# A ViT tower on one core: other tokenizer groups, masked remainder rows, and a hand-ordered start of the linear attention

## The chip, the cores and the metric

The kernel is written for one NeuronCore of a Trainium2 chip and runs on that core alone. The metric is the device time of one execution in microseconds (us). An execution has several engines that each take their instructions in order: TensorE (PE, with its weight loads listed as PEld), VectorE (DVE), ScalarE (ACT), GpSimd (POOL) and SyncE (SP), which issues most of the transfers; they wait for each other through semaphores.

## The reference, cut to what matters

Four images give 784 tokens of 256 numbers each, all in fp32. The tokens pass a tokenizer and two pre-norm layers, each of attention and a mixture of experts; each part is added to its input `h`.

```
# tokenizer
t = layernorm(layernorm(patches) @ W1 + b1)
h = silu(layernorm([t, t, t] @ Wp1 + bp1)) @ Wp2 + bp2
# layer 0: softmax attention, then top-2 of 6 experts
h = h + attention0(layernorm(h));  h = h + experts0(layernorm(h))
# layer 1: linear attention
q, k, v = split(layernorm(h) @ W_qkv + b_qkv), q and k centred
q2 = q*q / (sum(q*q) + 1e-7), then divided by its norm over the channels
k2 = k*k / (sum(k*k) + 1e-7), then divided by its norm over the TOKENS of the image
kv = k2^T @ v;  h = h + (v + q2 @ kv / sqrt(N)) @ W_out + b_out
# layer 1: shared MLP and top-2 of 4 experts
h = h + mlp1(layernorm(h))
```

The images in the output are written three times over (REP = 3). The norm of k2 over the tokens and `kv` are sums over all 784 tokens of one image: these are the sums that the change touches.

## The kernel before

**Rows.** An image is 784 = 6 * 128 + 16 rows. Its six full tiles of 128 rows are tiles 0 to 23 for the four images together; the four remainders of 16 rows share one more tile, LT = 24, the "left" tile, image b at partitions 32*b to 32*b + 15. The rows between hold values that belong to no token.

**Order.** The code records operations; a scheduler then places them on the engines. Inside `manual_schedule(engines=...)` the named engines keep the order of the code, and only there; operations recorded later, outside such a block, may still be put between those of the block. PSUM is a pool of 7 banks, and `copy_out` (L82) and `bias_relu` (L90) give their work in turn to ACT and DVE, by one counter that both share.

**Tokenizer (36 to 111 us).** It goes through the tiles in groups (L305): the first has tiles 0, 1, 2 and LT, seven more have three tiles each. For a group, `first_steps` (L537) multiplies the patches by Wall (`pw`, L547), copies half of the result to y on ACT (L550), takes statistics on DVE (L551), a square root on ACT (L556), y times r plus bp1 on DVE (L562), statistics, a second square root on ACT (L569) and the normalised rows xn on DVE (L573). `turned_rows` (L579) transposes xn on PE (`pt`, L274) and applies silu on ACT (L585). `last_rows` (L602) multiplies by Wp2 (`pwp`, L294) and adds the bias into h. `tokenize` (L594) takes these as a pipeline: group g's first steps, g - 1's turn, g - 2's last rows. The last group and the one before it are put in a fixed order on DVE, PE and ACT (from L634), and the layer norm of the next layer for the first group (`second_norm`, L615) is recorded ahead of the last groups. Silu and square root use different tables of ACT, so that the trace has a row ACT_TABLE_LOAD at each switch.

**Layer 1, linear attention (476 to 612 us).** The rows are units: units 0 to 7 have three tiles each, two units an image, and unit LU = 8 is the left tile. The outputs of layer 0's experts lie in DRAM (`yrows`). `fetch` (L1522) gathers them: for each tile two gathers, issued by POOL, into a buffer `ys` of which there are three. `stats_one` (L1539) waits for the two gathers, multiplies them by the routing weights, adds them to h (two DVE operations, L1545) and takes statistics (L1554, L1555). `normalise` (L1557) writes the normalised rows xa (L1568). `x_t` transposes xa (lxT, copied out by L86 and L88). `q_k` (L1734) multiplies by W_qkv (`pqk`, L1750), adds the bias on DVE (L1754) and squares on ACT. `scales` (L1765) computes the scale of each row and applies it to k on ACT (uk) and to q on DVE (L1781). `fold` (L1788) sums the squares of uk. `q_t` transposes the scaled q (lqT). `k_x` (L1809), once an image, sums over the image's tokens on PE: `pn` (L1816, L1817) for the norm, and `pukx`, uk transposed times xa, as two groups of six matmuls over the full tiles (L1829) and one over the image's 16 rows of the left tile (L1833). Their scaled result g (L1837) is transposed (`g_t`), multiplied by Wv·Wout (`kv_out`, L1853), and `rows_out` (L1867) adds the unit's result to h (`pout`, L1874, L1879). `layer1_weights` (L712) makes the products of the weights that this needs, and a bias `bout` that `residual` (L1575) adds to h.

The gathers for units 0, 1, LU and 2 are recorded inside the expert loop before, those for 3 and later in the loop from L1902, which takes the units in a software pipeline. That loop is left to the scheduler.

**Layer 1, mixture of experts (612 us to the end).** Four groups of four tiles and three of three; the matmuls `ps1`, `pe1`, `pe2`, `ps3` with relus by `bias_relu`, and the output transfers of each tile.

Of the kernel before, what the change touches and what calls it, by code (L numbers as in the profile page):

```python
# [27 lines left out]
P = 128  # L28
TT = 128
# [36 lines left out]
def tile_vit_tower(ctx: ExitStack, tc: tile.TileContext, a: dict, out: bass.AP):  # L66
# [59 lines left out]
    nc.gpsimd.memset(live, 0.0)  # L126
    for b in range(NI):
        nc.gpsimd.memset(live[b * SEG : b * SEG + LEFT], 1.0)

# [176 lines left out]
    groups[0].append(LT)  # L306

# [229 lines left out]
    def first_steps(g):  # L537

        tiles = groups[g]
        n = len(tiles)  # L540
        y = tokp.tile([TT, GT, D], F32, tag="y", name="y", bufs=2)
        st = small.tile([TT, GT, 6], F32, tag="st", name="st")
        mv = small.tile([TT, GT, 2], F32, tag="mv", name="mv")
        for j in range(n):
            pm = ps_tile("pw1")[:TT]
            for c in range(2):
                nc.tensor.matmul(  # L547
                    pm, pixels(c, tiles[j]), Wall[:, c, :], start=(c == 0), stop=(c == 1)
                )
            nc.scalar.copy(y[:, j, :], pm[:, D:])  # L550
            nc.vector.bn_stats(st[:, j, :], pm[:, :D])  # L551
            nc.vector.bn_aggr(mv[:, j, :], st[:, j, :])
        r = small.tile([TT, GT], F32, tag="rstd", name="rstd")[:, :n]
        nc.vector.tensor_tensor(r, mv[:, :n, 0], mv[:, :n, 0], ALU.mult)
        nc.vector.tensor_tensor(r, r, mv[:, :n, 1], ALU.add)
        nc.scalar.activation(r, r, AF.Sqrt, bias=zero[:TT])  # L556
        nc.vector.reciprocal(r, r)
        yield
        st = small.tile([TT, GT, 6], F32, tag="st", name="st")
        mv = small.tile([TT, GT, 2], F32, tag="mv", name="mv")  # L560
        for j in range(n):
            nc.vector.scalar_tensor_tensor(  # L562
                y[:, j, :], y[:, j, :], r[:, j : j + 1], bp1, ALU.mult, ALU.add
            )
            nc.vector.bn_stats(st[:, j, :], y[:, j, :])
            nc.vector.bn_aggr(mv[:, j, :], st[:, j, :])
        yield
        r = small.tile([TT, GT], F32, tag="rstd", name="rstd")[:, :n]
        nc.scalar.activation(r, mv[:, :n, 1], AF.Sqrt, bias=eps[:TT])  # L569
        nc.vector.reciprocal(r, r)  # L570
        xn = tokw.tile([TT, GT, D], F32, tag="xn", name="xn", bufs=3)
        for j in range(n):
            nc.vector.tensor_scalar(  # L573
                xn[:, j, :], y[:, j, :], mv[:, j, 0:1], r[:, j : j + 1],
                ALU.subtract, ALU.mult,
            )
        normed[g] = xn

    def turned_rows(g):  # L579
        xn = normed.pop(g)  # L580
        n = len(groups[g])
        xT = tokw.tile([P, 2, GN], F32, tag="xTt", name="xTt")

        def put(c, pt):
            nc.scalar.activation(  # L585
                xT[:, c, : n * TT], pt, AF.Silu, scale=col("lnp_g", c), bias=col("lnp_b", c)
            )

        transposed(xn, n, put)
        return xT  # L590
# [3 lines left out]
    def tokenize(g):  # L594
        if g < len(groups):
            first_rows(g)
        if 1 <= g <= len(groups):
            third[g - 1] = turned_rows(g - 1)
        if g >= 2:
            last_rows(g - 2)  # L600

    def last_rows(g):  # L602
        sT = third.pop(g)
        tiles = groups[g]
# [23 lines left out]
    n = len(groups)  # L628
# [83 lines left out]
    def layer1_weights():  # L712
        WvT = w1p.tile([P, 2, D], F32, tag="WvT", name="WvT")
        pt = ps_tile("pwv").rearrange("p (k i) -> p k i", k=2)
        for k in range(2):
            for c in range(2):
# [3 lines left out]
                )  # L720
        nc.vector.tensor_copy(WvT, pt)
        Wvo = w1p.tile([P, 2, D], F32, tag="Wvo", name="Wvo")
# [8 lines left out]
        bvs = w1p.tile([P, 2, P], F32, tag="bvs", name="bvs")  # L731
        for k in range(2):
            nc.vector.tensor_copy(bvs[:, k, :], col("bv", k).to_broadcast([P, P]))
# [7 lines left out]
        return Wvo, bvo, bres  # L741
# [775 lines left out]

    for xa in (*xas, xaL):
        nc.gpsimd.memset(xa[:, :, D : D + 2], 1.0)
# [37 lines left out]
    def normalise(u):  # L1557
        if u >= len(units):
            return
        b, j0, n = units[u]  # L1560
        t0 = b * TPI + j0
        st, mv = stats.pop(u)
        r = small.tile([TT, GT], F32, tag="rstd", name="rstd")
        nc.scalar.activation(r[:, :n], mv[:, :n, 1], AF.Sqrt, bias=eps[:TT])
# [7 lines left out]
        if lw:  # L1572
            residual(u)

# [6 lines left out]
    def x_t(u):  # L1581
# [7 lines left out]
        transposed(xa_of(u), n, lambda c, pt: copy_out(xT[:, c, : n * TT], pt))  # L1589
# [144 lines left out]
    def q_k(u, j0, j1):  # L1734

        n = units[u][2]
        xT = xTs[u]
        if j0 == 0:
# [4 lines left out]
            )  # L1743
        qk = qks[u]
        ss, s4 = sumsof[u]
        junk = lin.tile([TT, D], F32, tag="junk", name="junk", bufs=1)
        for j in range(j0, min(j1, n)):
            pqk = ps_tile("pqk")[:TT]
            for c in range(2):
                nc.tensor.matmul(  # L1750
                    pqk, xT[:, c, cut(j, 1)], Wqkv[:, c, : 2 * D],
                    start=(c == 0), stop=(c == 1),
                )
            nc.vector.tensor_tensor(qk[:, j, :], pqk, bqkv[:, : 2 * D], ALU.add)  # L1754

            for i in range(2):
                half = qk[:, j, i * D : (i + 1) * D]
                nc.scalar.activation(half, half, AF.Square, accum_out=ss[:, j, i : i + 1])  # L1758
            nc.scalar.activation(junk, qk[:, j, :D], AF.Square, accum_out=s4[:, j : j + 1])
            if 0 < u < LU - 1:  # L1760
                stats_one(u + 1, j)
        if j1 >= n and 0 < u < LU - 1:
            normalise(u + 1)

    def scales(u):  # L1765

        b, j0, n = units[u]
        qk = qks[u]
        ss, s4 = sumsof.pop(u)

        nc.vector.tensor_scalar(ss[:, :n], ss[:, :n], 1e-7, None, ALU.add)
        nc.scalar.activation(s4[:, :n], s4[:, :n], AF.Sqrt, bias=zero[:TT])
# [3 lines left out]
        nc.vector.reciprocal(ss[:, :n], ss[:, :n])  # L1776
        uk = uks[u] = own_of(lin, u, [TT, UT, D], "uk", 3)
        sq = own_of(lin, u, [TT, UT, D], "sq", 1)
        for j in range(n):
            nc.scalar.activation(uk[:, j, :], qk[:, j, D:], AF.Copy, scale=ss[:, j, 1:2])  # L1780
            nc.vector.tensor_scalar(  # L1781
                qk[:, j, :D], qk[:, j, :D], ss[:, j, 0:1], None, ALU.mult
            )
        for j in range(n):
            nc.scalar.activation(sq[:, j, :], uk[:, j, :], AF.Square)
        return sq

# [11 lines left out]
    def q_t(u):  # L1799
# [7 lines left out]
        transposed(qks.pop(u), n, lambda c, pt: copy_out(qT[:, c, : n * TT], pt))  # L1807

    def k_x(b):  # L1809

        acc = sums.pop(b)
        own = slice(b * SEG, b * SEG + LEFT)
        pn = psum_s.tile([P, 512], F32, tag="pss", name="pn")
        for c in range(2):
            of_c = slice(c * P, (c + 1) * P)
            nc.tensor.matmul(pn[:, c : c + 1], acc[:, of_c], ones[:TT], start=True, stop=False)  # L1816
            nc.tensor.matmul(  # L1817
                pn[:, c : c + 1], squares[LU][own, 0, of_c], ones[own], start=False, stop=True
            )
        kn = small.tile([P, 2], F32, tag="kn", name="kn")  # L1820
        nc.scalar.activation(kn, pn[:, :2], AF.Sqrt, scale=float(REP), bias=zero)
        nc.vector.tensor_scalar(kn, kn, 1e-12, None, ALU.max)
        nc.vector.reciprocal(kn, kn)
        g = gs[b] = lin.tile([P, 2, D + 2], F32, tag="g", name="g")
        for c in range(2):
            pg = ps_tile("pukx")[:, : D + 2]
            for j in range(TPI):
# [4 lines left out]
                )  # L1832
            nc.tensor.matmul(  # L1833
                pg, uks[LU][own, 0, c * P : (c + 1) * P], xaL[own, 0, : D + 2],
                start=False, stop=True,
            )
            nc.vector.tensor_scalar(  # L1837
                g[:, c, :], pg, kn[:, c : c + 1], REP / math.sqrt(REP * SEQ),
                ALU.mult, ALU.mult,
            )  # L1840

# [61 lines left out]
    for u in range(LU + 2):  # L1903
        b, odd = divmod(u - 2, 2)
        one_image = u >= 2 and not odd
        if u == 0:
            fetch(3)
            x_t(1)
            q_k(0, 0, UT)
            squares[0] = scales(0)  # L1910
            fold(0, squares.pop(0))
            continue
# [7 lines left out]
        if u == 2:  # L1920
            gT = g_t(0)
            kv_out(0, gT)
            rows_out(0)
            x_t(2)
        if u == 1:
            stats_one(LU, 0)
            normalise(LU)
        if u < LU:
            q_k(u, 0, 2)
        if u == 1:  # L1930
            x_t(LU)
        if one_image and b:
            gT = g_t(b)
        if u < LU:
            q_k(u, 2, UT)
            if u == 1:
                q_k(LU, 0, 1)
                lw.extend(layer1_weights())
                Wvo, bvo = lw[:2]
            squares[u] = scales(u)  # L1940
            if u == 1:
                squares[LU] = scales(LU)
                q_t(LU)
        if one_image and b:
# [5 lines left out]
        if 2 <= u < LU - 1:  # L1950
            x_t(u + 1)
        if u == 3:
            for k in (0, 1, 2, LU):
                residual(k)
        if u >= 2 and (b or odd):
            rows_out(u - 2)
# [109 lines left out]
```

## Time and profile before

| what | value |
|---|---|
| runs of the kernel | 783.15, 783.83, 780.32 us; median 783.15 |
| the profiled execution's own time | 784.6 us |
| its span in the trace | 782.9 us |
| mean granted clock of TensorE | 0.965 |

The profile is of one execution. A page of it has the busy time of each engine, the span in 40 slices, the chain of work that ended last, and the costliest groups of instructions. From the trace come further views: the waits of a stretch (who waited for whom, in all, how often, and the longest), the timeline of an engine (start, duration, engine, line, operation, output <- inputs, count, and in brackets the idle time before it with what ended it), and a table of windows (each engine's busy time and instructions in a stretch, then the granted clock, the share of DMA engines busy, and GB/s). Instructions of one engine overlap a little in the trace: a row of 0.48 us may start 0.40 us after the one before, so that sums of rows are made with the distance between starts where it is known.

### The profile page before, as it was taken

How to read it: one execution, taken by the hardware profiler on the slowest of the kernel's cores; microseconds unless marked ns; L12 is line 12 of the kernel's file. 1: busy time of each engine (PE TensorE's matmuls, PEld its weight loads, DVE VectorE, ACT ScalarE, POOL GpSimd, SP SyncE). 2: the span in 40 equal slices, each digit the busy share in tenths (PEclk: the TensorE clock that was granted, in tenths of full speed). 3: DMA queues.
4: the chain of work that ended last, by engine and by line, in shares of the span. 5: the costliest groups of instructions: out<-in, count | busy, mean ns of one | idle time of the engine just before them, and what ended most of it. 6: DMA issues, size and time to landing. Idle time of an engine off the chain costs nothing.

```text
span 782.9 us, 10611 instructions
## 1 busy us (share of the span) xinstructions
PE 722.2 (92%) x3408; PEld 496.6 (63%) x3408; DVE 483.2 (62%) x1519; ACT 338.3 (43%) x787; POOL 127.7 (16%) x217
## 2 busy tenths in 40 slices
PE   7888889999888779999999998699999999999996
PEld 4745455666555458888888884566676775554653
DVE  4676776778779763456446666789855545444441
ACT  0547875554663654342223325416445612222221
POOL 5300000000073407600033004770000000000000
PEclk9899999999999689999999999799999999999999
DMA  8399999000020663433244324330000013223333
GB/s 205 88 418 417 418 418 412 5 0 1 0 75 33 239 232 121 162 108 90 87 137 131 99 79 129 102 95 20 1 0 2 1 23 96 82 64 100 104 108 108
DMA packets 57749, 98.07 MB, mean 125 GB/s; under 512 B 6407, under 2 KB 47598, under 8 KB 57694
## 3 DMA queue, kind: packets, MB, share of 16 engines
q1 hardware_dynamic: 51184, 80.96, 29.2%
q0 software_dynamic: 5632, 14.58, 6.1%
q10 hardware_dynamic: 878, 1.86, 1.0%
q8 instruction: 27, 0.44, 0.2%
q14 instruction: 28, 0.23, 0.1%
HBM read 31.50 MB, written 65.88 MB: 124 GB/s over the span
## 4 chain that ended last, share of the span: by engine, by line
PE 72%; DVE 16%; ACT 8%; issue 2%; DMA 1%; POOL 0%; DVEq 0%; ACTq 0%; POOLq 0%
PE pb L1321 13%; PE pyb L1338 6%; PE pe L283 6%; PE ps L283 4%; PE pqk L1750 4%; PE pkv L283 4%; PE pt L274 4%; PE pukx L1829 3%; PE ps L2016 3%; PE pout L1874 3%; PE pout L1879 3%; DVE oT L842 3%; PE pwp L294 2%; PE pwo L294 2%; PE ptp L344 2%
## 5 line engine op out<-in xcount | busy, mean ns | idle before, releaser
L1031 POOL DMA_INDIRECT xrows<-xn,pos x50 | 56.4, 1128 | 245.9 <-ACT kq L782 191.0
L1531 POOL DMA_INDIRECT ys<-yrows,pos x52 | 52.8, 1015 | 145.6 <-DMA yrows<-yb 130.6
L1321 PE MATMUL pb<-xTb,own 128*128 128x256 f32 x240 | 59.0, 390 | 3.4 <-DVE r L891 1.8
L1327 ACT ACTIVATE hb<-pb,own 128x256 f32<-128x256 f32 x74 | 35.1, 475 | 55.3 <-PE pb L1321 48.6
L1321 PE MATMUL pb<-hb,own 128*128 128x256 f32 x240 | 57.0, 380 | 0.3 <-DVE hb L1329 0.3
L1338 PE MATMUL pyb<-own,hb 128*128 128x256 f32 x240 | 57.1, 380 | 0.0
L1321 PEld LDWEIGHTS pb<-xTb,own 128*128 128x128 f32 x240 | 44.7, 194 | 11.8 <-issue 1.9
L274 PE MATMUL pt<-ident,xn 128*128 128x128 f32 x200 | 33.9, 296 | 17.6 <-DVE xn L573 11.1
L1338 PEld LDWEIGHTS pyb<-own,hb 128*128 128x128 f32 x240 | 45.4, 190 | 6.5 <-ACT hb L1327 0.4
L1750 PE MATMUL pqk<-Wqkv,lxT 128*128 128x512 f32 x100 | 46.5, 611 | 0.9 <-ACT lxT L86 0.9
L1321 PEld LDWEIGHTS pb<-hb,own 128*128 128x128 f32 x240 | 43.4, 190 | 5.9 <-DVE hb L1329 0.7
L274 PEld LDWEIGHTS pt<-ident,xn 128*128 128x128 f32 x200 | 25.1, 149 | 34.0 <-ACT y L550 10.4
L1344 DVE TENSOR_TENSOR yb<-pyb,eb 128x512 f32<-128x512 f32 x30 | 20.7, 691 | 41.2 <-PE pyb L1338 41.2
L283 PE MATMUL pe<-xT,eW 128*128 128x512 f32 (+1 forms) x112 | 46.0, 553 | 0.0
L1311 ACT COPY xTb<-ptb 128x512 f32<-128x512 f32 x30 | 17.5, 584 | 63.4 <-PE ptb L1307 63.4
L547 PE MATMUL pw<-Wall,pT 128*128 128x512 f32 x96 | 42.8, 593 | 0.0
L1329 DVE TENSOR_SCALAR hb<-pb,own 128x256 f32<-128x256 f32 x46 | 22.1, 482 | 28.7 <-PE pb L1321 28.6
L807 DVE SCALAR_TENSOR_TENSOR prod<-kq 128x784 f32<-128x784 f32 x32 | 30.4, 972 | 6.0 <-ACT kq L1165 3.4
L283 PEld LDWEIGHTS pe<-xT,eW 128*128 128x128 f32 x112 | 20.2, 190 | 21.6 <-issue 16.5
L1750 PEld LDWEIGHTS pqk<-Wqkv,lxT 128*128 128x128 f32 x100 | 18.7, 194 | 22.0 <-issue 17.3
L1298 DVE COPY own<-ew 128x1540 f32 x30 | 29.0, 965 | 4.9 <-issue 1.6
L1758 ACT ACTIVATE qk<-qk 128x256 f32<-128x256 f32 x50 | 20.3, 407 | 23.7 <-DVE qk L1754 21.4
(394 smaller groups left out, 1481.2 us busy)
## 6 DMA issues: line engine op xcount, KB each, us to landing
xrows<-nothing SPq DMA_DIRECT2D x22, 896.0 KB
yrows<-nothing SPq DMA_DIRECT2D x22, 896.0 KB
out_dram<-h SPq DMA_DIRECT2D x23, 384.0 KB
xb<-xrows SPq DMA_DIRECT2D x30, 256.0 KB
yrows<-yb SPq DMA_DIRECT2D x30, 256.0 KB
ew<-in_L_ffn_expert_w_dram SPq DMA_DIRECT2D x6, 768.0 KB
wb<-wd SPq DMA_DIRECT2D x16, 128.0 KB
img<-in_x_dram SPq DMA_DIRECT2D x2, 588.0 KB
```

Source lines behind the costliest of these rows:

```text
L274: nc.tensor.transpose(pt[:, j * TT : (j + 1) * TT], xn[:, j, c * P : (c + 1) * P], ident[:TT, :TT])
L283: nc.tensor.matmul(pm[: wcols.stop - wcols.start, :n], w[:, c, wcols], xT(c), start=(c == 0), stop=(c == chunks - 1),)
L294: nc.tensor.matmul(pm[:, i, :], xT(c, t), w[:, c, :], start=(c == 0), stop=(c == chunks - 1))
L547: nc.tensor.matmul(pm, pixels(c, tiles[j]), Wall[:, c, :], start=(c == 0), stop=(c == 1))
L807: nc.vector.scalar_tensor_tensor(prod, qTs[s][:, o, :], 1.0, kT[:, o, t * SEQ : (t + 1) * SEQ], ALU.mult, ALU.mult, accum_out=atts[s][:, o ...
L1031: put = nc.gpsimd.indirect_dma_start(out=xrows[:, :], out_offset=bass.IndirectOffsetOnAxis(ap=pos[:, k, t0 + j : t0 + j + 1], axis=0), in_ ...
L1298: nc.vector.tensor_copy(w, ewf[0][:, bass.ds(off, EW)])
L1321: nc.tensor.matmul(pm, wm[:, c, o * P : (o + 1) * P], src[:, c, :], start=(c == 0), stop=(c == 1),)
L1327: nc.scalar.activation(dst[:, o, :], pm, AF.Relu, bias=b)
L1338: nc.tensor.matmul(pm[:, t, :], src[:, c, t * P : (t + 1) * P], wm[:, c, :], start=(c == 0), stop=(c == 1),)
L1531: got = nc.gpsimd.indirect_dma_start(out=y[:, j, k, :], out_offset=None, in_=yrows[:, :], in_offset=bass.IndirectOffsetOnAxis(ap=pos[:, k, ...
L1750: nc.tensor.matmul(pqk, xT[:, c, cut(j, 1)], Wqkv[:, c, : 2 * D], start=(c == 0), stop=(c == 1),)
```

## The change

It has three parts.

**Tokenizer.** The tiles are taken in seven groups, `turns`: 0, 1, 2 and LT; three groups of four tiles (3 to 6, 7 to 10, 11 to 14); three groups of three (15 to 23). The normalisation behind it (`second_norm`) keeps the old groups.

**Remainder rows.** A constant `ofimage` [128, 4] is 1 in column b at the 16 rows of image b, else 0; five small POOL memsets make it. A new tile xaM holds four copies of the left tile's xa, each multiplied by one column of `ofimage`, on POOL. The left matmuls of `pukx` then use all 128 rows of uk's left tile against xaM, and those of `pn` all 128 rows of the squares against the column of `ofimage`.

**Order of the linear attention's start.** The functions are split into smaller steps. Units 0, 1, LU and the start of 2 and 3 are written out in a fixed order for DVE, PE and ACT; POOL is not in that order. The loop starts at unit 3. The transposed left tile is always copied out by DVE, and `residual` is put off for the units normalised before the weights are there.

```diff
+    ofimage = const.tile([P, NI], F32, tag="ofimage", name="ofimage")
+    nc.gpsimd.memset(ofimage, 0.0)
     for b in range(NI):
         nc.gpsimd.memset(live[b * SEG : b * SEG + LEFT], 1.0)
+        nc.gpsimd.memset(ofimage[b * SEG : b * SEG + LEFT, b : b + 1], 1.0)
...
+    turns = [[0, 1, 2, LT], *([t, t + 1, t + 2, t + 3] for t in (3, 7, 11))]
+    turns += [[t, t + 1, t + 2] for t in (15, 18, 21)]
...
-        tiles = groups[g]
+        tiles = turns[g]
...
-        transposed(xa_of(u), n, lambda c, pt: copy_out(xT[:, c, : n * TT], pt))
+        copy = nc.vector.tensor_copy if u == LU else copy_out
+        transposed(xa_of(u), n, lambda c, pt: copy(xT[:, c, : n * TT], pt))
...
+    def k_x_left(b):
+        for c in range(2):
+            nc.tensor.matmul(
+                pgxs[b, c], uks[LU][:, 0, c * P : (c + 1) * P], xaM[:, b, :],
+                start=False, stop=True,
+            )
...
-                pn[:, c : c + 1], squares[LU][own, 0, of_c], ones[own], start=False, stop=True
+                pn[:, c : c + 1], squares[LU][:, 0, of_c], ofimage[:, b : b + 1],
+                start=False, stop=True,
...
-            nc.tensor.matmul(
-                pg, uks[LU][own, 0, c * P : (c + 1) * P], xaL[own, 0, : D + 2],
-                start=False, stop=True,
-            )
...
-    for u in range(LU + 2):
...
+    steps = layer1_weights()
+    with tc.manual_schedule(engines=by_hand):
+        x_t(1)
+        for j in range(UT):
+            qk_mm(0, j)
+            qk_add(0, j)
+            qk_squares(0, j)
+        root(0)
+        for j in range(UT):
+            qk_mm(1, j)
+        qk_add(1, 0)
+        qk_squares(1, 0)
+        stats_one(LU, 0)
+        norm_root(LU)
+        factors(0)
+        qk_add(1, 1)
+        qk_squares(1, 1)
+        norm_rows(LU)
+        for b in range(NI):
+            nc.gpsimd.tensor_scalar(
+                xaM[:, b, :], xaL[:, 0, : D + 2], ofimage[:, b : b + 1], None, ALU.mult
+            )
+        fetch(3)
+        fetch(4)
+        qk_add(1, 2)
+        qk_squares(1, 2)
+        root(1)
+        q_rows(0)
+        next(steps)
+        x_t(LU)
+        q_t(0)
+        k_rows(0)
+        next(steps)
+        stats_one(2, 0)
+        factors(1)
+        q_rows(1)
+        k_rows(1)
+        qk_mm(LU, 0)
+        next(steps)
+        Wvo, bvo = lw[:2]
+        q_t(1)
+        qk_add(LU, 0)
+        qk_squares(LU, 0)
+        root(LU)
+        stats_one(2, 1)
+        stats_one(2, 2)
+        fetch(5)
+        norm_root(2)
+        squares[0] = k_squares(0)
+        factors(LU)
+        fold(0, squares.pop(0))
+        norm_rows(2)
+        k_rows(LU)
+        squares[LU] = k_squares(LU)
+        q_rows(LU)
+        squares[1] = k_squares(1)
+        fold(1, squares.pop(1))
+        k_x_tiles(0)
+        x_t(2)
+        k_x_left(0)
+        kn = k_norm(0)
+        k_x_out(0, kn)
+        qk_mm(2, 0)
+        qk_add(2, 0)
+        qk_squares(2, 0)
+        stats_one(3, 0)
...
+        kv_out(0, gT)
+        qk_squares(2, 2)
+        stats_one(3, 2)
+        normalise(3)
+        rows_out(0)
+        x_t(3)
+    squares[2] = scales(2)
+    fold(2, squares.pop(2))
+    for u in range(3, LU + 2):
```

The order of the built program, which the diff does not show, is this on two engines. On POOL, counted from the last write of the experts' rows: gathers for LU (2), unit 2 (6), unit 3 (6), the first of unit 4, then the four xaM operations, then unit 4's other five, two for the left tile once more (as before), and units 5, 6 and 7. On DVE, the scheduler has put operations of the loop between those of the block: between `stats_one(2, 0)` and `q_rows(1)` stand the six additions of unit 4's gathered rows to h (L1545 in the numbers of before), and between `q_rows(1)` and `kv_out(0)` the additions for units 5, 6 and 7.

## The prediction, on record before the changed kernel ran

> **What bounds the kernel now.** I read the page first, then the windows of the three stretches that the change touches, then timelines there.
>
> ```profile
> span 782.9 us, 10611 instructions
> PE 722.2 (92%) x3408; PEld 496.6 (63%) x3408; DVE 483.2 (62%) x1519; ACT 338.3 (43%) x787; POOL 127.7 (16%) x217
> PE 72%; DVE 16%; ACT 8%; issue 2%; DMA 1%; POOL 0%; DVEq 0%; ACTq 0%; POOLq 0%
> ```
>
> PE is busy for 92% and the last chain runs through it for 72%: a change gains only where PE stands idle, or gets shorter work. Such places are the tokenizer and the start of the linear attention. The windows' columns are stretch, length, busy PE, PEld, DVE, ACT, POOL, granted clock, DMA share, GB/s:
>
> ```profile
> 476.00:506.00 30.00, 21.07 (x63) 12.32 (x62) 22.22 (x73) 17.28 (x68) 21.72 (x23) 0.85 0.33 97
> 506.00:531.00 25.00, 23.78 (x93) 16.50 (x92) 20.96 (x54) 5.60 (x22) 19.00 (x18) 0.91 0.33 96
> 530.00:547.00 17.00, 16.70 (x73) 11.69 (x71) 15.88 (x52) 11.59 (x44) 0.18 (x1) 1.00 0.04 11
> ```
>
> From 476 to 506 PE is idle 8.9 us, from 506 to 531 1.2 us; from 530 it is full, and the window 547 to 612 has 65.00 us of PE in 65.00. Whatever is late at 530 stays late to the end.
>
> **Tokenizer groups: -3.0 us.** The waits of 36 to 130 us (total, times, longest) hold `PE pt <- DVE xn` for 11.1 us in 7 waits, singly 1.89, .85, 1.11, 1.38, 1.11, 1.94, 2.82. What is late is ACT:
>
> ```profile
> 69.50 1.28 ACT L585 ACT_TABLE_LOAD   x1 [2.00 <-PE pt L274]
> 70.79 0.67 ACT L585 ACTIVATE xTt<-pt,cols 128x384 f32<-128x384 f32 x1
> 71.48 1.28 ACT L556 ACT_TABLE_LOAD   x1
> 72.78 0.30 ACT L556 ACTIVATE rstd<-rstd,zero 128x3 f32<-128x3 f32 x1
> 73.09 1.28 ACT L585 ACT_TABLE_LOAD   x1
> 74.39 0.67 ACT L585 ACTIVATE xTt<-pt,cols 128x384 f32<-128x384 f32 x1
> ...
> 75.61 1.28 ACT L569 ACT_TABLE_LOAD   x1
> 76.91 0.30 ACT L569 ACTIVATE rstd<-mv,eps 128x3 f32<-128x3 f32 x1
> ```
>
> A group of three has four table loads, however many tiles it holds: 4 x 1.28 + 2 silu x .67 + 2 roots x .30 + .64 of copies = 7.7, and reciprocal .2 and the first xn .35 follow before PE may go on. PE's work for it is 12 `pw` (5.31), 6 transposes and 12 `pwp` (3.28), some 8.6 us of a period of 9.7 to 10.0. A fourth tile adds a third of the latter, 2.8, and little to ACT (a copy .35, longer silu): PE 11.4 against a chain of about 10.4, so PE sets a group of four. I walked the seven new groups in the built order: idle times of 0.4 (the fourth tile's 1.7 of `pw` fill the 1.89), 2.6 (ACT has the root of group 1 behind the four y copies of group 2: last copy 58.7, load 1.28, root .3, reciprocal .2, xn .35 give 60.95, where `pw` ends at 58.35), 0, 0.95, 1.55, 1.65: 7.2 for 11.1, a gain of 3.9. At the end a table load and root of the last group stand behind the first copy of layer 0's transposes in ACT's order, and xn is 0.9 later: net -3.0. Bounds: the gaps move to later groups unchanged and the 0.9 is lost (+0.9); or four of seven gaps and the clock's loss after them go (-6).
>
> That loss is seen at 110.70: after the 2.82 idle the 12 `pwp` took 4.44, elsewhere 2.32. [...]
>
> **Sums over whole arrays: -1.0 us.** A pair of left matmuls over 16 rows takes 0.63 between starts, a pair over 128 rows 2.80 / 6 = 0.467:
>
> ```profile
> 581.66 0.70 PE L1833 MATMUL pukx<-xaL,uk 16*128 16x258 f32 x2
> 582.29 2.88 PE L1829 MATMUL pukx<-xa,uk 128*128 128x258 f32 x12
> ```
>
> .16 x 2 pairs x 3 images in which PE is full = 1.0 (nothing, if a first use of xaM's column costs as much, to 1.3 with all four images). `pn` has the same .31 per pair in both forms: 0. The five new memsets (128x6 takes .10 on POOL) stand at the start behind DVE's and ACT's long work: 0; uncovered, 0.5.
>
> **The fixed order with the moved additions: +10.7 us.** In the built DVE order the six additions of unit 4 stand between the first ones of unit 2 and `q_rows(1)`. Each waits for a gather of its own, and POOL gives out the gathers one by one:
>
> ```profile
> 477.57 0.96 POOL L1531 DMA_INDIRECT ys<-yrows,pos  x1 [48.13 <-DMA yrows<-yb]
> 478.83 0.95 POOL L1531 DMA_INDIRECT ys<-yrows,pos  x1 [0.30 <-issue]
> ...
> 495.27 0.95 POOL L1531 DMA_INDIRECT ys<-yrows,pos  x1 [0.30 <-DVE ss L1773]
> ...
> 502.12 0.96 POOL L1531 DMA_INDIRECT ys<-yrows,pos  x1 [0.30 <-issue]
> ```
>
> One each 1.26 us, from 477.57, when the last rows are in DRAM; the additions that wait for the first two run at 480.37 and 481.65, 2.8 after their issue. 495.27 is the 15th, unit 4's first; 502.12 is its last. Between them the changed POOL has xaM, four operations 128x258. No row has this one on POOL: a memset 128x256 takes .31, 128x6 .10, 128x1792 1.6. I take 0.5 each, near the row of its own size, 2.0 in all (bounds 0.4 to 6.4). Unit 4's last gather so goes at 504.1 and lands at 506.9; its addition (.45) and three `q_rows` (.9) end at 508.4.
>
> ```profile
> 496.64 1.01 DVE L1781 TENSOR_SCALAR qk<-qk,ss 128x256 f32<-128x256 f32 x3
> ```
>
> Before, this was done at 497.6. DVE, which runs its instructions in order, reaches unit 4's first addition at about 489 and then stands for 18 us. Queued behind are `q_rows(1)`, unit 1's lqT, LU's bias, unit 2's other additions: all that PE needs next. PE runs dry near 492.
>
> From 508.4 DVE is the bound. To unit 0's kvo the built order has 22 additions x .40 = 8.8, three residuals 2.15, 9 statistics 3.1 and 8 aggregations .7, copies 1.9, four biases 2.4, five `acc` 1.7, xa .96, q of LU .3, g .86, kvo .8, small ones .5: 24.2 us. Added to these are waits of some 2.7, since unit 5's gathers take unit 4's buffer and so start at 507.9, and the first of unit 7 land by 527 ahead of g. kvo is then ready at 535.3. `pout` of unit 0, unit 3's transposes and copy follow (before: kvo 516.1 ahead of 517.97, and so on): 6.0 to the first `pqk` of unit 3 at 541.3. Before, with the same work done:
>
> ```profile
> 530.58 0.70 PE L1750 MATMUL pqk<-Wqkv,lxT 128*128 128x512 f32 x1 [0.30 <-ACT lxT L86]
> ```
>
> That is +10.7. The additions of units 5 to 7, done early, relieve DVE later (18 x .40 = 7.2), but there PE is full and nothing comes back. Bounds: +6.4 with no waits after 508 and xaM at 0.4; +16.3 with xaM at 6.4 and landings of 4.0, the longest here. The relus of the experts change engines by the shared counter: 0, PE isn't idle there.
>
> **Sum.** 784.6 - 3.0 - 1.0 + 10.7 = 791.3 against the profiled execution. That lay 1.4 above the median of the runs, 783.15: I predict 790 us. All low ends give 784.6 - 6 - 1.3 + 6.4 - 1.4 = 782.3, all high ends 784.6 + 0.9 + 16.3 - 1.4 = 800.4.
>
> **Rivals.**
>
> *POOL is slower still* (0.11). xaM at its upper bound and landings of 4.0 put unit 4's last addition 4.4 + 1.2 later: about 795. For it: POOL has few rows of this kind. Against: its 128x256 row takes .31.
>
> *The delay is regained* (0.20). Additions done early leave DVE 7.2 us more room after 530, and the delay of 10.7 shrinks to some 4: 784.6 - 3.0 - 1.0 + 4.0 - 1.4 = 783.2 to 785. For it: DVE is busy 15.88 of 17 us in the window from 530, so that it is nearly a bound there. Against: PE is busy 16.70 in it and has no gap in the next 65 us.
>
> *Unit 4's rows don't hold DVE* (0.07), the side of faster. The point that decides is whether they have landed when DVE reaches them, 488.8. Then `q_rows(1)` would come at 493.0, 15.4 earlier than I have it, the first `pqk` of unit 3 at about 526.5 (-4.1), as 8.9 us of PE's idle time would be partly filled: 784.6 - 3.0 - 1.0 - 4.1 - 1.4 = 775. For it: the fixed order does close PE's idle time from 476 to 506. Against: the 20th gather can't be issued 13 us sooner at POOL's pace.
>
> **How the numbers follow.** My forecast has 0.62, for 787 to 798 or so; worse 0.11, regained 0.20, faster 0.07. The range leaves out the faster case and the far end of the worse: 782 to 799. A measurement of this kernel tells some 0.5% from no change, 779.2 to 787.1. Faster: 0.07. Within: regained and the forecast's lowest edge, 0.21. Slower: 0.72.
>
> **What would show it.** In the changed profile the `DVE h <- DMA ys` waits near 490 to 507 should sum to 14 us or more, against 3.5 from 476 to 540 before; PE should have an idle time of over 10 us near 492 to 507 and a lower clock after it; the first `pqk` of unit 3 should stand near 541 less the 3 from the tokenizer. xaM rows of POOL should be 0.5 each. In the tokenizer, `PE pt <- DVE xn` should sum to about 7, with 22 table loads up to the first layer. A left pair of `pukx` should take 0.47. I'm wrong if DVE's wait is under 5 us, or if PE shows gaps after 541 that the delay can fill.

## The result and the profile after

| | kernel before | changed kernel |
|---|---|---|
| median of 19 runs each | 784.19 us | 788.58 us |
| ratio, 95% interval | | 1.0056 (1.0039 to 1.0073) |
| profiled execution, its span | 784.6, 782.9 | 788.72, 787.0 |
| end of the tokenizer (first `ptable`) | 115.07 | 110.25 |
| first gather after the experts' last rows | 477.57 | 472.83 |
| from there to the first `pqk` of unit 3 | 53.0 | 66.8 |
| from there to the end of the span | 252.3 | 247.3 |

The change costs 4.4 us by the medians, 4.1 in the profiled executions: 4.7 won up to the first gather, 13.8 lost in the start of the linear attention, 5.0 won behind it. The page of the changed kernel:

```profile
span 787.0 us, 10609 instructions
PE 716.8 (91%) x3408; PEld 495.9 (63%) x3408; DVE 483.3 (61%) x1515; ACT 331.8 (42%) x777; POOL 128.5 (16%) x226
PE 70%; DVE 14%; ACT 5%; DMA 5%; POOL 3%; issue 2%; SPq 1%; DVEq 0%; ACTq 0%; POOLq 0%
```

PE works 5.4 us less, and the kernel takes longer. In the chain that ended last DMA and POOL, 1% and 0% before, now hold 5% and 3%: the chain goes through the gathers. The waits of DVE from 476 to 540 us (total, times, longest) say where. First the kernel before, then the changed one:

```profile
DVE h L1545 <- DMA ys<-yrows,pos: 3.5, 5, 1.6
```

```profile
DVE h L1554 <- DMA ys<-yrows,pos: 17.3, 9, 9.0
```

The timelines of the changed kernel's POOL, DVE and PE show the wait from three sides:

```profile
490.48 0.95 POOL L1540 DMA_INDIRECT ys<-yrows,pos  x1 [0.30 <-issue]
491.46 3.95 POOL L1992 TENSOR_SCALAR xaM<-xaL,ofimage 128x258 f32<-128x258 f32 x4
495.57 1.00 POOL L1540 DMA_INDIRECT ys<-yrows,pos  x1 [0.16 <-issue]
...
500.65 0.95 POOL L1540 DMA_INDIRECT ys<-yrows,pos  x1 [0.30 <-issue]
```

```profile
493.22 1.13 DVE L1554 SCALAR_TENSOR_TENSOR h<-ys,wk,h 128x256 f32<-128x256 f32 x2 [9.04 <-DMA ys<-yrows,pos]
498.48 0.49 DVE L1554 SCALAR_TENSOR_TENSOR h<-ys,wk,h 128x256 f32<-128x256 f32 x1 [4.13 <-DMA ys<-yrows,pos]
...
503.53 0.48 DVE L1554 SCALAR_TENSOR_TENSOR h<-ys,wk,h 128x256 f32<-128x256 f32 x1 [0.77 <-DMA ys<-yrows,pos]
503.93 0.87 DVE L1824 TENSOR_SCALAR qk<-qk,ss 128x256 f32<-128x256 f32 x3
```

```profile
486.52 1.03 PE L744 MATMUL pbvo<-Wout,bvs 128*128 128x256 f32 x4
504.43 1.55 PE L277 MATMUL pt<-ident,qk 128*128 128x128 f32 x6 [16.88 <-DVE qk L1824]
505.77 7.05 PE L1869 MATMUL pukx<-xa,uk 128*128 128x258 f32 x24
517.25 1.76 PE L277 MATMUL pt<-ident,xa 128*128 128x128 f32 x6 [4.44 <-DVE xa L1588]
...
539.67 5.42 PE L1770 MATMUL pqk<-Wqkv,lxT 128*128 128x512 f32 x12 [0.24 <-ACT lxT L86]
```

On POOL unit 4's first gather goes at 490.48, then the masks take 3.95 us, and its last gather goes at 500.65. On DVE the first addition of unit 4 waits 9.04 us for that first gather, the next 4.13 for the gather behind the masks, and the last runs at 503.53, 2.9 us after its gather was issued. `q_rows(1)` (L1824) stands behind it, and PE has nothing to do for 16.88 us. The windows (stretch, length, busy PE, PEld, DVE, ACT, POOL, granted clock, DMA share, GB/s) add what follows:

```profile
488.00:504.00 16.00, 0.00 (x0) 0.00 (x0) 4.20 (x13) 1.21 (x3) 13.36 (x14) 0.63 0.29 80
504.00:531.00 27.00, 21.34 (x66) 14.43 (x66) 22.25 (x65) 8.78 (x34) 18.48 (x19) 0.72 0.33 94
```

After the idle time PE has a clock of 0.72: its 24 `pukx` take 7.05 us.

### The profile page after: what moved, and what is told of

Its sections match the earlier page's. It is cut to its first block, busy times and chain, and to the rows that moved or that the text cites. A ratio compares the mean times of both kernels' runs of the same rounds, so it can differ in the third digit from the quotient of the medians.

```text
span 787.0 us, 10609 instructions
## 1 busy us (share of the span) xinstructions
PE 716.8 (91%) x3408; PEld 495.9 (63%) x3408; DVE 483.3 (61%) x1515; ACT 331.8 (42%) x777; POOL 128.5 (16%) x226
## 4 chain that ended last, share of the span: by engine, by line
PE 70%; DVE 14%; ACT 5%; DMA 5%; POOL 3%; issue 2%; SPq 1%; DVEq 0%; ACTq 0%; POOLq 0%
PE pb L1329 13%; PE pyb L1346 6%; PE pe L286 6%; PE pqk L1770 5%; PE ps L286 4%; PE pt L277 4%; PE pkv L286 4%; PE pw L552 3%; PE pwp L297 3%; PE ps L2144 3%; PE pout L1944 3%; PE pout L1949 3%; PE pukx L1869 2%; DVE prod L815 2%; PE pe L2114 2%
## 5 line engine op out<-in xcount | busy, mean ns | idle before, releaser
L1039 POOL DMA_INDIRECT xrows<-xn,pos x50 | 54.6, 1091 | 242.4 <-ACT kq L790 186.2
L1554 DVE SCALAR_TENSOR_TENSOR h<-ys,wk,h 128x256 f32<-128x256 f32 x50 | 23.5, 484 | 17.7 <-DMA ys<-yrows,pos 17.3
```

Source lines behind the costliest of these rows:

```text
L1039: put = nc.gpsimd.indirect_dma_start(out=xrows[:, :], out_offset=bass.IndirectOffsetOnAxis(ap=pos[:, k, t0 + j : t0 + j + 1], axis=0), in_ ...
```

## The experiments

The kernels were run on three chips, each beside the kernel before on the same chip. On the first the kernel before took 809.09 us, on the others 784.54 and 784.27. The first chip's traces hold long waits whose releaser the trace calls "remote", which the traces of before and after don't have. These are two of them from the kernel with the sums over 16 rows:

```profile
ACT lxT L86 <- remote: 13.4, 1, 13.4
DVE lxT L88 <- remote: 10.3, 1, 10.3
```

So the first four kernels were run again on the other chips, and the argument rests on those second runs. The first are given with their ratio to 809.09, but the "remote" waits differ from kernel to kernel, and a ratio there need not be that of another chip: the kernel with the sums over 16 rows has 0.9964 there and 1.0108 on another chip. Since the tokenizer's end moved by up to 2.7 us between the traces with the new groups (108.52 to 111.17), the stage is measured by its own length, from the first gather behind the last rows to the first `pqk` of unit 3 (before 53.0, changed 66.8).

**The groups alone.** The kernel before with `turns` in the tokenizer:

```diff
+    turns = [[0, 1, 2, LT], *([t, t + 1, t + 2, t + 3] for t in (3, 7, 11))]
+    turns += [[t, t + 1, t + 2] for t in (15, 18, 21)]
...
-        tiles = groups[g]
+        tiles = turns[g]
```

> The kernel before with the tokenizer's new groups and nothing else. Theory: the tokenizer's end (the table transposes, 115.07 us before, 110.25 after) comes 4.4 to 4.8 us earlier and stays so to the end, because PE is nearly full from there on: about 779.7 us beside 784.2, ratio 0.994. Rival: the gain is given back in the wait for the last experts' rows or in the start of the linear attention, which in the kernel before has idle PE too: 784, ratio 1.000.

> The kernel before with the new groups alone, a second time: in its first trace ACT and DVE stood 10.0 and 13.2 us in the linear attention's start on waits for which the trace names no releaser of this core ('remote'), which the traces of before and after don't have. Theory: without such waits 4.4 to 4.8 us under the kernel before, 0.994. If the waits come again, their sum is above 20 us and the kernel before on the same chip is near 809 again.

Measured 803.47 beside 809.09, ratio 0.9929 (0.9900 to 0.9957), and the second time 778.97 beside 784.54, ratio 0.9936 (0.9908 to 0.9964), without "remote" waits; the stage has 52.9 us, as before. So the groups bring 5 us, as expected, and nothing takes them back.

**The additions held behind kvo.** The additions of units 4 to 7 get a dependency, without a semaphore, on unit 0's kvo; POOL keeps its order, masks included:

```diff
-            nc.vector.scalar_tensor_tensor(
+            added = nc.vector.scalar_tensor_tensor(
                 h[:, t, :], ys[u][:, j, k, :], wk[:, k, t : t + 1], h[:, t, :],
                 ALU.mult, ALU.add,
             )
+            if 4 <= u < LU:
+                tc.add_manual_dep(
+                    added.ins, held[0].ins.name,
+                    mybir.DependencyInfo(mybir.DependencyClass.NoSync, mybir.DependencyReason.DATA),
+                    reason="after",
+                )
```

> The changed kernel, with the additions of the gathered rows of units 4 to 7 kept behind unit 0's kvo on DVE. Theory (the moved additions make DVE, and PE behind it, wait for POOL's gathers): the 16.9 us of idle PE before the transposes of unit 1's q shrink to 4 or less, the first product of unit 3 comes at about 522 us (515 to 526) instead of 539.7, and the time is about 772 us (766 to 779). Rival (the fixed order itself is the loss, the waits are hidden by work that must be done anyway): 786 to 789, with the idle time at another place.

> The changed kernel with the additions of units 4 to 7 kept behind unit 0's kvo, a second time, for the same reason. Theory: the idle time of PE before the transposes of unit 1's q is 4 us or less, the first product of unit 3 starts 48 us after the first gather that follows the last rows (66.8 in the changed kernel, 53.0 before), and the time is 772 to 776 beside a kernel before of 784. Rival (the fixed order is itself the loss): 53 us or more, and 785.

> The changed kernel with the additions held behind kvo, a third look without timing rounds, for the spread of the stretch between the first gather and unit 3's first product: 42.8 us within 0.5, if nothing but the order sets it.

Measured 788.03 beside 809.09, ratio 0.9739 (0.9708 to 0.9770); again 770.47 beside 784.54, ratio 0.9834 (0.9792 to 0.9876); the third, a single run, 774.77. PE of the second run:

```profile
485.89 0.82 PE L277 MATMUL pt<-ident,qk 128*128 128x128 f32 x6
486.54 5.39 PE L1876 MATMUL pukx<-xa,uk 128*128 128x258 f32 x24
494.77 1.31 PE L277 MATMUL pt<-ident,xa 128*128 128x128 f32 x6 [2.84 <-DVE xa L1595]
...
514.10 5.42 PE L1777 MATMUL pqk<-Wqkv,lxT 128*128 128x512 f32 x12 [0.24 <-ACT lxT L86]
523.20 1.21 PE L277 MATMUL pt<-ident,xa 128*128 128x128 f32 x6 [3.68 <-DVE xa L1595]
```

No idle time stands before the transposes of unit 1's q, no wait for `ys` is left on DVE, and the stage has 42.8 us, 24.1 less than in the changed kernel and 10.3 less than before: a larger gain than the 48 us and the 772 to 776 us expected. The place of the additions is the loss, and not the fixed order. Of the 24.1 us, 17.8 are gone by the end of `q_rows(1)` (14.2 us after the first gather instead of 32.0), which are unit 4's additions with their waits; 6.4 more are gone between it and kvo, where DVE has 8 additions ahead of kvo instead of 22. The third run had 45.4 us, outside the half microsecond expected. Its trace differs from 497 on, after the same idle time, by PE's clock: 0.89 over the stage instead of 1.00.

**The masks on DVE.**

```diff
         for b in range(NI):
-            nc.gpsimd.tensor_scalar(
+            nc.vector.tensor_scalar(
                 xaM[:, b, :], xaL[:, 0, : D + 2], ofimage[:, b : b + 1], None, ALU.mult
             )
```

> The changed kernel, with the four masking operations on DVE instead of POOL, at the same place of the fixed order, where DVE has 9 us of waiting behind it. Theory (POOL's pace of gathers sets the end of DVE's wait): the 3.95 us of masking between the first and second gather of unit 4 go, the later gathers come 4.1 us earlier, and so do the q of unit 1, kvo and the end: 784.5 us, 4 below the changed kernel. Rival (after the wait DVE's own work is the bound, and the additions of units 5 to 7 don't wait): 1 us or less.

> The changed kernel with the masking on DVE, a second time. Theory (POOL's pace sets the end of DVE's wait): the idle time of PE before unit 1's transposes falls from 16.9 to 13 us, the first product of unit 3 comes 62.7 us after the first gather instead of 66.8, and the time is 784.5. Rival: 66 us and 788.

Measured 802.15, ratio 0.9904 (0.9872 to 0.9936); again 785.03 beside 784.54, ratio 1.0003 (0.9988 to 1.0017). DVE's masks and PE's idle time in the second run:

```profile
481.58 1.20 DVE L1992 TENSOR_SCALAR xaM<-xaL,ofimage 128x258 f32<-128x258 f32 x4
501.65 1.55 PE L277 MATMUL pt<-ident,qk 128*128 128x128 f32 x6 [11.85 <-DVE qk L1824]
```

PE's idle time is 11.85 us, the stage 63.0, near the 13 and 62.7 expected. A mask takes 0.35 us on DVE, where it is hidden, and 0.99 on POOL, where it stands ahead of five gathers: 3.9 us of the stage are the masks' place.

**The additions held behind q_rows(1) only.** The same dependency on unit 1's last `q_rows`:

```diff
+        if u == 1:
+            held.append(got)
```

> The changed kernel with the additions of units 4 to 7 kept behind q_rows(1) only, not behind kvo. Theory (the wait for unit 4's gathers is the loss, wherever it stands ahead of unit 2's additions and kvo): the same 5 to 9 us of waiting for gathers stand a few instructions later, PE does unit 1's transposes and the first sums earlier, and the first product of unit 3 gains 1 us or less: 787.5. Rival (what costs is that q_rows(1) is late): the gain is most of that of the additions held behind kvo, 774 to 778.

Measured 783.50 beside 784.54, ratio 1.0001 (0.9979 to 1.0022); the stage has 62.7 us, 4.1 less. The expectation was a gain of 1 us or less, and its rival most of the gain of the additions held behind kvo: neither size is right. PE shows why:

```profile
485.48 5.39 PE L1878 MATMUL pukx<-xa,uk 128*128 128x258 f32 x24
510.58 1.77 PE L277 MATMUL pt<-ident,xa 128*128 128x128 f32 x6 [19.71 <-DVE xa L1595]
```

The idle time is still 19.71 us, only later: unit 2's additions and its xa now stand behind the wait. But the 24 `pukx` are done before it, in 5.39 us instead of 7.05; they took 5.39 too in the second run held behind kvo, whose granted clock was 1.00 over the stage. So the wait costs wherever it stands ahead of unit 2's rows, as the theory had it, and a part depends on what PE can still do meanwhile.

**The sums over 16 rows back.** The masks are still made, and not used:

```diff
-                pgxs[b, c], uks[LU][:, 0, c * P : (c + 1) * P], xaM[:, b, :],
+                pgxs[b, c], uks[LU][own, 0, c * P : (c + 1) * P], xaL[own, 0, : D + 2],
...
-                pn[:, c : c + 1], squares[LU][:, 0, of_c], ofimage[:, b : b + 1],
+                pn[:, c : c + 1], squares[LU][own, 0, of_c], ones[own],
```

> The changed kernel, with the sums over 16 rows of the left tile as before; the masked tile is still made, and not used. Theory from the traces of before and after (the distance between the same instructions of images 1, 2 and 3 shrank by 1.0 us each): 3 us longer, 791.6. Rival (0.16 per pair of the left matmuls alone, as predicted): 1.0 longer, 789.6.

> The changed kernel with the sums over 16 rows of the left tile as before, a second time, since the first trace had waits of 6.5 to 13.4 us on ACT and DVE without a releaser of this core. Theory (each image that PE does at full load gained 1.0 us): 791.6 beside a kernel before of 784.2, and the distance from the first product of unit 3 to the end grows from 247.3 to 250.3. Rival (0.33 per image, as predicted): 789.6 and 248.3.

Measured 806.50, ratio 0.9964 (0.9946 to 0.9982), on the first chip; again 791.94 beside 784.27, ratio 1.0108 (1.0060 to 1.0156), where the changed kernel has 1.0056. The time is the one expected, though the two intervals overlap, so that the traces must show the difference. Their account isn't the one expected: from unit 3's first `pqk` to the end are 249.4 us, 2.0 more than in the changed kernel and not 3.0; the other 1.4 are in the stage before it (68.2), which the edit touches for one image; why it is as much as that was not tried. Image 3 of this kernel and of the changed one:

```profile
624.53 0.28 PE L1889 MATMUL pn<-ones,acc 128*128 128x1 f32 x2
...
625.66 5.49 PE L1869 MATMUL pukx<-xa,uk 128*128 128x258 f32 x24
631.08 1.13 PE L1877 MATMUL pukx<-xaL,uk 16*128 16x258 f32 x4
632.14 0.87 PE L277 MATMUL pt<-ident,qk 128*128 128x128 f32 x6
```

```profile
621.21 0.28 PE L1887 MATMUL pn<-ones,acc 128*128 128x1 f32 x2
...
622.01 5.47 PE L1869 MATMUL pukx<-xa,uk 128*128 128x258 f32 x24
627.32 1.03 PE L1876 MATMUL pukx<-xaM,uk 128*128 128x258 f32 x4
628.19 0.82 PE L277 MATMUL pt<-ident,qk 128*128 128x128 f32 x6
```

By the starts `pn` takes 0.80 instead of 1.13, the four left matmuls 0.87 instead of 1.06, and the 24 `pukx` between them 5.31 instead of 5.42: 0.63 an image, 1.9 of the 2.0 us for three. In the kernel before, where the left matmuls stood in two pairs, each behind its full tiles, they took 1.26.

**Held unit by unit.** Two kernels that keep the additions of unit u + 1 behind unit u's normalised rows from unit 4 on; unit 4's own behind unit 0's g in the first, behind its kvo in the second:

```diff
+                    added.ins, held[u].ins.name,
...
+        if u >= 4:
+            held[u + 1] = got
...
+        if b == 0:
+            held[4] = got
```

> The changed kernel with the additions of unit 4 kept behind unit 0's g, and those of unit u + 1 behind the normalised rows of unit u from unit 4 on. Theory: the 3.7 us idle time of PE before unit 4's transposes, which the additions held behind kvo left, and the lower clock after it go, unit 0's kvo comes 1 to 2 us later: 767 to 769. Rival (the additions of unit 4 ahead of kvo wait for their gathers again): 774 or more.

> As the one before, with unit 4's additions behind unit 0's kvo. Theory: as in the additions held behind kvo up to unit 3's first product (42.8 us after the first gather), then unit 4's normalised rows come some 2 us earlier, since three of unit 5's additions no longer stand ahead of them: 767 to 769. Rival (the residual additions set it): 770.5, no change.

The first takes 764.06 us beside 784.27, ratio 0.9758 (0.9712 to 0.9805): 20 us under the kernel before, the best here, and 3 us better than the 767 to 769 expected. The second takes 771.42, ratio 0.9868 (0.9811 to 0.9925), no better than all held behind kvo: its rival holds, for the idle time before unit 4's transposes is 3.42 us, hardly less than 3.68. In the first it is gone:

```profile
511.31 1.99 PE L1940 MATMUL pkvo<-Wvo,gT 128*128 128x256 f32 x8 [1.22 <-ACT gT L1931]
...
519.38 5.42 PE L1779 MATMUL pqk<-Wqkv,lxT 128*128 128x512 f32 x12 [0.24 <-ACT lxT L86]
524.63 0.82 PE L277 MATMUL pt<-ident,xa 128*128 128x128 f32 x6
```

So unit 4's additions belong between unit 0's g and its kvo: late enough for their gathers, for which DVE no longer waits, and early enough for xa.

## Why the prediction was right

**The mechanism** is shown: additions that the scheduler put ahead of `q_rows(1)` wait for POOL's gathers, and holding them back takes 24.1 us out of the stage. Measured from the first gather, `q_rows(1)` ends at 32.0 us, by the prediction at 30.8. PE's idle time is 16.88, where the prediction has PE dry from near 492 to the end of `q_rows(1)` at 508.4. The built order was told too wide in one point: of the 18 additions of units 5 to 7, the trace has 14 ahead of kvo, and the last four run at 552.92 to 556.36. With unit 2's four and unit 3's first four these are the 22 that the prediction counts.

**The masks** were taken at 0.5 us each and measured 0.99, inside the bounds. The row chosen, a memset 128x256, took 0.31: it was no guide to the masks, which also read and multiply and took 0.99.

**From `q_rows(1)` to kvo** the prediction has 26.9 us with DVE as the bound, 24.2 of work and 2.7 of waits; the trace has 29.3 (504.80 to 534.12), of which DVE is busy 24.5. So the work was right, and the waits are 4.8: 1.7 for gathers, and 2.9, which the prediction left out, for PE and for ACT behind it. PE's clock after the idle time, named among the things to look for and not priced, makes PE later: 7.05 for 24 `pukx` instead of 5.39, 5.68 for the first 8 `pqk` of unit 2 instead of 3.68 where the additions are held (granted clock 0.72 from 504 to 531 here, 1.00 over the stage there). How much of the 2.9 is the clock was not tried apart. The stage lost 13.8 us where the prediction had 10.7.

**"Nothing comes back"** failed: 5.0 us came back behind unit 3's first `pqk`. Not by the rival's way, through a DVE relieved of its additions, for PE has no gap there before or after that could close. From that `pqk` to the last image's `pkvo` are 95.5 us in the kernel before, 93.8 in the one with the groups alone, 92.5 with the new order and 16-row sums, 90.5 in the changed kernel. The first step, 1.7, is the clock. The same 12 `pukx`, first in the profiled execution of before, then with the groups alone:

```profile
547.09 4.56 PE L1829 MATMUL pukx<-xa,uk 128*128 128x258 f32 x12
```

```profile
543.08 2.88 PE L1831 MATMUL pukx<-xa,uk 128*128 128x258 f32 x12
```

From 547 to 552 the kernel before has a granted clock of 0.66 while PE is busy 5.00 of 5.00 us. A PE that is busy all the time thus still had time to give back, which "there PE is full and nothing comes back" denies. The order is the same in both kernels there, and why one lost its clock is open: for the forecast this 1.7 is luck. The second, 1.3, goes with the new order, which puts the four left matmuls together; how much of it is that was not tried apart. The third, 2.0, is the masked sums.

**The sums** were put at -1.0 and give -2.0 in the three images: the step that failed most is "`pn` has the same .31 per pair in both forms". A pair over 128 rows takes 0.22 from start to start in the changed kernel, and the 0.31 before was measured with 16-row pairs between them.

**The tokenizer** was put at -3.0 and gave -4.2 at the first scatter of layer 0's experts (217.49 to 213.30), -4.7 at the first gather, -5 as a time of its own. The walk through the groups held: idle times of 0.18, 2.82, 0, 1.11, 1.26 and 1.19 for 0.4, 2.6, 0, 0.95, 1.55 and 1.65; 6.6 in all for 7.2. ACT's table loads between 30 and 130 us fell by four, from 25 to 21. The loss of 0.9 at its end was 0.5 (PE's wait for xn of 0.72 instead of 0.24), and the first `pw` came 0.36 earlier, with which the change has nothing to do. The clock's loss at 110.70 was taken too large: the 2.32 us "elsewhere" are rows of 10 `pwp`, and 12 took 2.76 in the changed kernel, so that it was 1.7 us (granted clock 0.61 before, 1.00 there).

**A rival, priced too low.** *Unit 4's rows don't hold DVE* put the first `pqk` of unit 3 at -4.1. With the additions of units 4 to 7 held back, which is more than that rival had, it comes 10.3 us earlier in the stage than before: the fixed order is worth more than the prediction gave it.

That the time came so near is in part luck. The tokenizer was 1.7 us better than its term, what came back was 4.0 better, the start of the linear attention 3.1 worse, and these nearly cancel. The time lay 1.4 under the forecast, 788.58 for 790; against the 784.19 of the larger number of runs, 1.0 above the 783.15 that the forecast started from, the change cost 4.4 us where 6.9 were forecast.

## What to carry to other kernels

When an order is written by hand and the rest is left to a scheduler, look at the built order of each engine for operations from outside that stand inside, and ask of each what it waits for: an addition that was harmless behind its gather stops a whole engine ahead of it, here DVE for 9.04 us at the first of unit 4. A cheap operation on the engine that issues the gathers can cost its own time on the gathers behind it: the four masks took 3.95 us of POOL, unit 4's second gather went 5.09 us after its first where two gathers in the kernel before are 1.26 apart, and the masks' place was 3.9 us of the stage. An idle time of PE is priced with the slow work that can follow it, and not by its length alone: the two runs below differ by 2.6 us in the stage after the same 2.85 us.

## What the runs showed of the hardware

After the same idle time of 2.85 us PE sometimes keeps its clock, and sometimes not. The same place in two kernels whose order is the same up to there, first unit by unit behind kvo, then the third run of all held behind kvo:

```profile
494.93 1.31 PE L277 MATMUL pt<-ident,xa 128*128 128x128 f32 x6 [2.85 <-DVE xa L1595]
```

```profile
497.05 1.76 PE L277 MATMUL pt<-ident,xa 128*128 128x128 f32 x6 [2.85 <-DVE xa L1595]
```

The granted clock of the stage was 1.00 in the one and 0.89 in the other, and the stage took 42.8 and 45.4 us. The second run of all held behind kvo kept its clock at this place after 2.84 us (1.31 us for the six transposes, 1.00 over the stage), and the one held behind unit 0's g lost it after 2.85 (1.76 us for the same six, 0.89). So in these four runs the length of the idle time alone doesn't decide it; what does was not shown.

The kernel before took 809.09 us on one chip and 784 on the others. The waits that the trace calls "remote" are seen only there; what they wait for stays open. So does why the kernel before and the one with the groups alone are 24.5 us slower there than on another chip, and the three with the hand-written order only 14.6 to 17.6.
